# A first and a last batch with forms of their own, and new moments, in a four-layer graph network on one core

## The chip, the core and the metric

The kernel runs on one core of one Trainium2 chip. Five engines take part, each with a queue that it works through in order: PE (TensorE, matmuls), DVE (VectorE), ACT (ScalarE), POOL (GpSimd) and SP (SyncE, which here only issues transfers). Transfers are carried out by 16 DMA engines. The metric is the device time of one execution in microseconds (us), before the change 2229.95 us in the median of three runs.

## The reference

Sixteen batches of 1024 nodes with 64 channels pass through four graph layers. Each layer adds its result to its input and normalises over the channels:

```python
x = _layernorm(x + _L0_gnn_ref(x, adj, L0_gnn_weight, L0_gnn_bias), axis=-1)
x = _layernorm(x + _L1_gnn_ref(x, adj, L1_gnn_theta), axis=-1)
x = _layernorm(x + _L2_gnn_ref(x, adj, nodemask, L2_gnn_W1, ...), axis=-1)
x = _layernorm(x + _L3_gnn_ref(x, adj, L3_gnn_gamma, ...), axis=-1)
```

- Layer 0 is `adj @ (x @ weight) + bias`.
- Layer 1 is a Chebyshev sum of order four: `z0 = x`, `z1 = adj @ x`, `z(k) = 2 adj @ z(k-1) - z(k-2)`, each times its own `theta[k]`.
- Layer 2 drops some neighbours of nodes with many of them (`_dilate_adj`), sorts the remaining neighbours' values channel by channel, takes the quantiles 0.25, 0.5 and 0.75 by linear interpolation, weights and adds them, and sends the sum with `x` through a small perceptron (64 to 128 to 64).
- Layer 3 normalises over all batches and nodes at once, multiplies by `W`, and subtracts the product with `sqrt(d) * adj * rsqrt(d)`, where `d` are the row sums of `adj`.

About 0.8% of the adjacency is set, so a node has some nine neighbours. The kernel ranks the nodes by their number of neighbours, so that few nodes need a long sort.

## The kernel before

Nodes lie on the 128 partitions, eight groups of 128 to a batch (NK = 8). A batch goes through nine generators, each a function with `yield`s that cut it into steps:

- `rows_in` (11 steps): loads the adjacency in eight tiles of 128 rows (L405, SP's queue, two buffers), makes of each a key (ACT's Sign, L539, times a band on DVE, L541) whose eight largest per block (MAX8, L544) give the list of neighbours; `transposed` (L410 to L416) turns the tile on PE and ACT copies it into the transposed adjacency `f_adj_t`. After the last tile that adjacency is written out (4 MB, L565) and the first product with it is made.
- `layers` (13): layers 0 and 1. Layer 0's norm is eight squares with sums on ACT (L366), a root on ACT (L369), a reciprocal on DVE (L371, `n1_r`) and eight scalings on ACT (L376). Products with the adjacency are `hop2` (L385 to L396), 16 matmuls that the profile shows as 32 rows; ACT copies the result out (`f_ct`, L602). The last product's rows go to DRAM (`rows`, L630), from where they are gathered.
- `lists` (15): neighbours, gaps and ranks on DVE (L646 to L739), then for each of the eight groups a comparison (`at16`, L747) and the matmuls that place the lists (L751) and reorder the batch's own rows (L515, `reordered`); then ACT copies out `ids`, `more` and `meta` (L770 to L776) and the reordered rows (L785).
- `fetch` (15): 70 gathers per batch on POOL (L808), each followed by a memset (L811): 15 for class 0, 37 for class 1 and 18 for class 2.
- `heads` (10), three classes: nodes of one group with up to 24 slots (class 0), four groups with 11 (class 1), three with 8 (class 2). `dead` (L832) marks empty slots once the gathers have landed; ACT copies the gathered values into `home` and adds a huge number where the slot is empty (L880, 23, 40 and 21 instructions).
- `sorts` (141): a sorting network on DVE (L912) between the tiles `home` and `away`; then ACT multiplies the sorted slots by the quantile weights (L928) and PE adds them up (L929).
- `ends` (5): perceptron and layer 2's norm. Its product is scaled on ACT (L965), added on DVE (L966) and normalised as above (`n2`).
- `back` (11): brings the rows into the old order with eight comparisons on DVE (L993) and the matmuls of L515.
- `third` (5): the local part of layer 3. Step 1 turns the rows, copies them (L1011), takes statistics (bn_stats, L1014), multiplies by `rd` (L1019, `f_u`); step 2 is the product and ACT's copy of it (`f_ht`, L1025); steps 3 and 4 multiply by `sd` (L1030) and write out z (L1042).

A last stage over all batches (not in the diff) normalises and writes the output.

The order on the engines is written by hand. Each step has a due time in `WHEN`; step u of a part of batch b is due at `b * PERIOD + WHEN[part][u]` with PERIOD = 118, and all steps of all batches are sorted by that, ties in the order in which they were listed, which is by batch:

```python
parts += [(b * PERIOD + when, b, name, u, part) for u, when in enumerate(WHEN[name])]
for _, b, name, u, part in sorted(parts, key=lambda p: p[0]):
    next(part)
```

The due times are no times of the chip; they only settle the order in which instructions are put on the queues. Three or four batches are under way at once: batch b's tiles and its layers run while batch b-2 is sorted and batch b-3 is in `third`. A setup of weights and constants (`prepared`, L447 to L497) is cut into pieces that run after steps named in SETUP.

Of the kernel before, what the change touches and what calls it, by code (L numbers as in the profile page):

```python
# [10 lines left out]
F32 = mybir.dt.float32  # L11
BF16 = mybir.dt.bfloat16
F16 = mybir.dt.float16
# [3 lines left out]
ALU = mybir.AluOpType  # L17
# [25 lines left out]
SETUP = (("rows in", 8), ("rows in", 10), ("layers", 1))  # L43
# [135 lines left out]
def _strides(slots):  # L179

    out, rest = [], list(slots)
    while rest:
# [16 lines left out]
    "rows in": (-307.2, -238.7, -234, -231.9, -226.9, -224.5, -217, -214.8, -208.8, -202.9, -195.8),  # L199
    "layers": (-174.9, -126.5, -121.9, -119.7, -113.9, -113.5, -107.6, -104.6, -98.7, -96.7, -79.9, -79.6, -77.8),  # L200
    "lists": (-134.7, -132, -126.3, -126.3, -117.8, -76.3, -76.3, -74.6, -63.5, -63.4, -61.9, -57.9, -57.4, -45.7, -12.4),
    "fetch": (-18.6, -1.8, -1.8, 0.8, 0.8, 5.6, 24.5, 28.9, 28.9, 52.8, 56.1, 56.1, 79.5, 91.2, 92.5),
    "heads": (5.3, 15.7, 18.7, 67.9, 93.8, 93.8, 93.8, 115.1, 121.9, 126.8),
    "sorts": (
        23.2, 23.2, 23.2, 23.2, 23.2, 23.2, 23.2, 23.2, 23.2, 23.2, 23.2, 23.2, 24.8, 34.3, 38, 38.6, 38.7, 38.7,
        42.6, 42.6, 43.4, 43.4, 45.4, 45.4, 48.8, 49.7, 51, 51, 51.9, 51.9, 53.9, 55.5, 55.5, 55.5, 55.8, 57, 57,
        57, 57, 57, 57, 59.5, 59.5, 60.5, 61.9, 61.9, 61.9, 62.5, 62.5, 62.5, 62.5, 62.5, 62.5, 62.5, 62.5, 62.5,
        62.5, 62.5, 63.6, 63.6, 63.6, 68.3, 68.3, 70.5, 71.5, 73.4, 73.7, 77.1, 77.7, 79.1, 79.1, 79.1, 80.2, 80.2,
        89.2, 89.2, 93, 93.4, 93.4, 93.9, 102.3, 102.3, 102.3, 102.3, 102.3, 102.3, 109.8, 109.8, 110.3, 111.3,
        111.7, 111.9, 111.9, 111.9, 113.8, 113.8, 114.2, 114.2, 114.2, 114.4, 116.9, 117.4, 118.5, 118.6, 118.6,  # L210
        118.6, 118.6, 118.6, 118.6, 120, 121.7, 121.7, 121.7, 121.7, 121.7, 121.9, 121.9, 121.9, 121.9, 121.9,
        128.4, 128.4, 128.4, 128.4, 128.4, 128.4, 128.4, 128.4, 128.4, 128.9, 128.9, 128.9, 128.9, 133.1, 135.4,
        135.4, 135.4, 135.7, 135.7, 139.8, 140.7,
    ),
    "ends": (153.6, 155, 158.8, 173.2, 179),
    "back": (154.2, 174, 188, 189.1, 192.7, 197.9, 200.1, 209.6, 211.1, 212.5, 212.5),
    "third": (202.6, 227.3, 232.1, 236.9, 244.4),
# [4 lines left out]
def gnn_layers_kernel(  # L222
# [129 lines left out]
    def norm(wk, y, wholes, tag, centred=False):  # L352

        n = NK // len(wholes)
        part = lambda k: wholes[k // n][:, k % n, :]
        if not centred:
            s = wk.tile([P, NK], F32, name=f"{tag}_s")
            for i, t in enumerate(wholes):
                nc.vector.tensor_reduce(out=s[:, i * n : (i + 1) * n], in_=t, axis=AX.X, op=ALU.add)
            nm = wk.tile([P, NK], F32, name=f"{tag}_m")  # L360
            nc.vector.tensor_scalar(out=nm, in0=s, scalar1=-1.0 / C, scalar2=None, op0=ALU.mult)
        v = wk.tile([P, NK], F32, name=f"{tag}_v")
        for k in range(NK):
            sq = wk.tile([P, C], F32, name=f"{tag}_q")
            bias = 0.0 if centred else nm[:, k : k + 1]
            nc.scalar.activation(sq, part(k), AF.Square, bias=bias, scale=1.0, accum_out=v[:, k : k + 1])  # L366
        yield "square"
        sd = wk.tile([P, NK], F32, name=f"{tag}_d")
        nc.scalar.activation(sd, v, AF.Sqrt, bias=eps_s, scale=1.0 / C)  # L369
        rs = wk.tile([P, NK], F32, name=f"{tag}_r")  # L370
        nc.vector.reciprocal(rs, sd)  # L371
        if not centred:
            nc.vector.tensor_tensor(out=nm, in0=nm, in1=rs, op=ALU.mult)
        for k in range(NK):
            if centred:
                nc.scalar.mul(y[:, k, :], part(k), rs[:, k : k + 1])  # L376
            else:
                nc.scalar.activation(
                    y[:, k, :], part(k), AF.Identity, bias=nm[:, k : k + 1], scale=rs[:, k : k + 1]
                )  # L380
# [4 lines left out]
    def hop2(adj_t, v, ps):  # L385

        pairs = adj_t.rearrange("p j (q h n) -> p j h q n", h=2, n=P)
        for j in range(NK):
            for h in range(2):
                nc.tensor.matmul(  # L390
                    ps[h * C : (h + 1) * C, :],
                    lhsT=v[:, j, :],
                    rhs=pairs[:, j, h],
                    start=(j == 0),
                    stop=(j == NK - 1),
                )  # L396

    def turned(src, tag, bufs=1):

        pt = bank(tag, bufs)  # L400
        for q in range(NK // 2):
            nc.tensor.transpose(pt[:, q * P : (q + 1) * P], src[:, q * P : (q + 1) * P], ident)
        return pt

# [42 lines left out]
    def prepared(th, thp, mean, w0_c, left, mine, term):  # L447

        halves = [slice(h * C, (h + 1) * C) for h in range(2)]
        centred(mean, w0_c)  # L450
# [16 lines left out]
        nc.vector.tensor_copy(out=biases, in_=mine)  # L467
        yield

        nc.vector.tensor_copy(out=mask_f, in_=mask_u)  # L470
        pm = bank("end")
        nc.tensor.transpose(pm[:, 0:P], mask_f, ident)
        nc.vector.tensor_copy(out=mask_t, in_=pm[:, 0:P])
        nc.vector.tensor_copy(out=earlier, in_=earlier_f)
# [10 lines left out]
        centred(mean, thp)  # L485
        thf = bank("end").rearrange("p (k c) -> p k c", c=C)[:, 0:4]
# [36 lines left out]
    def rows_in(b, st, keyband, pa, pw):  # L523
# [7 lines left out]
        held = [load(b, i, pa) for i in range(2)]  # L531
        yield "load"
        for i in range(NK):
            a = held.pop(0)

            off = (NK - 1 - i) * P
            key = pa.tile([P, NK, P], F16, name="key", bufs=KEYS)
            flat_key = key.rearrange("p j n -> p (j n)")
            nc.scalar.activation(flat_key, a, AF.Sign)  # L539
            transposed(a, i, adj_t)  # L540
            nc.vector.tensor_tensor(out=flat_key, in0=flat_key, in1=keyband[:, off : off + N], op=ALU.mult)  # L541

            for j in range(NK):
                nc.vector.max(out=cand[:, i, j * 8 : j * 8 + 8], in_=key[:, j, :])  # L544
            left = cand[:, i, :]
            for r in range(KS // 8):
                top = lst[:, i, r * 8 : r * 8 + 8]
                nc.vector.max(out=top, in_=left)
                if r < KS // 8 - 1:
                    then = pa.tile([P, NK * 8], F16, name="then", bufs=2)  # L550
                    nc.vector.match_replace(out=then, in_to_replace=top, in_values=left, imm_value=0.0)
                    left = then
            if i + 2 < NK:
                held.append(load(b, i + 2, pa))
            yield f"tile{i}"
# [3 lines left out]
        q0 = bank("l0", 2)  # L559
        hop2(adj_t, x0, q0)  # L560
# [76 lines left out]
    def lists(b, st, pw):  # L637
# [105 lines left out]
        po = bank("px")  # L743
        pr, px = (pr[:, : NK * RW].rearrange("p (k s) -> p k s", s=RW), pr[:, NK * RW : (NK + 1) * RW])
        for k in range(NK):
# [21 lines left out]
            reordered(po, st["x_parts"], at_place[:, 0:N], k)  # L767
# [15 lines left out]
        yield "ids"  # L783
        own_t = pw.tile([P, N], F16, name="row").bitcast(F32)
# [32 lines left out]
    def heads(b, st, gots, pw, ps_):  # L817

        meta, xs = st["meta"], st["xs"]
        for ns, nr, _, ks in CLASSES:  # L820
# [50 lines left out]
            nc.scalar.copy(home[:, 0, :, :], xs[:, kk, :])  # L871
# [5 lines left out]
            for u, v in zip(cuts[:-1], cuts[1:]):  # L877
                for s in range(u, v):
# [10 lines left out]
    def sorts(b, st, ps_):  # L889

        xs = st["xs"]
        for (ns, nr, _, ks), (steps, homes) in zip(CLASSES, plans):
# [31 lines left out]
            for u, v in zip(*(np.linspace(0, nr, SUMS[k0] + 1).astype(int)[e] for e in (slice(0, -1), slice(1, None)))):  # L924
                for i in range(u, v):
                    t = home[homes[i]][:, i]
                    for k in range(nk):
                        nc.scalar.mul(t[:, k, :], t[:, k, :], wts[:, i, k : k + 1])  # L928
                    nc.tensor.matmul(total, lhsT=quarter, rhs=flat(t), start=False, stop=(i == nr - 1))  # L929
                yield f"sums{k0}"  # L930

    def ends(b, st, pw):
# [31 lines left out]
        for k in range(NK):  # L964
            nc.scalar.mul(h[:, k, :], ph[:, k * C : (k + 1) * C], meta[:, k, 1:2])  # L965
        nc.vector.tensor_tensor(out=h, in0=h, in1=xs, op=ALU.add)  # L966
        x3p = h
        yield from norm(pw, x3p, [h], "n2", centred=True)
# [3 lines left out]
    def back(b, st, pw):  # L972
# [4 lines left out]
        for g in range(2):  # L977
# [9 lines left out]
            nc.scalar.copy(row[:, g * 512 : (g + 1) * 512], ps)  # L987
            yield f"row{g}"
# [12 lines left out]
    def third(b, st, pa, pw):  # L1001
# [9 lines left out]
        nc.scalar.copy(flat(x3), turned(xt, "end"))  # L1011
        nc.sync.dma_start(out=x3_d[b], in_=flat(x3))
        st = pw.tile([P, 6], F32, name="f_st")
# [3 lines left out]
        u = pw.tile([P, NK, C], F32, name="f_u")  # L1017
        for k in range(NK):
            nc.scalar.mul(u[:, k, :], x3[:, k, :], rd[:, k : k + 1])  # L1019
        nc.scalar.copy(u[:, :, C - 1], rd)  # L1020
# [8 lines left out]
        for k in range(NK):  # L1029
            nc.scalar.mul(z[:, k, :], pq[:, k * C : (k + 1) * C], sd[:, k : k + 1])  # L1030
# [15 lines left out]
    with (  # L1046
# [28 lines left out]
        for b in range(B):  # L1075
            st = {}
            for name, part in (
# [10 lines left out]
                parts += [(b * PERIOD + when, b, name, u, part) for u, when in enumerate(WHEN[name])]  # L1088
# [691 lines left out]
```

## Time and profile before

| | us |
|---|---|
| three runs | 2225.72, 2229.95, 2231.18 |
| the profiled execution, its own time | 2228.49 |
| the profiled execution, its span | 2226.6 |
| first gather of batch 0 starts | 112.86 |
| first gather of batch 14 and of batch 15 | 1821.12, 1941.38 |
| last gather's memset | 2060.47 |
| last stage begins | about 2145 |

The granted TensorE clock of that execution was 0.857 on the mean. The page gives the busy time of each engine and, in 40 slices, its share in tenths. A line of the timeline has the start, the duration, the engine, the line and operation, the output and input tiles with their shapes, and in brackets the idle time just before, with what ended it. Lines of several like instructions in a row are put together (x8). In lists of waits the three numbers are the time in total, the number of times and the longest, in us. In tables of windows each engine has its busy time and the number of instructions, then come the granted PE clock, the DMA share and GB/s.

### The profile page before, as it was taken

The page shows a single profiled execution, that of the slowest core. Times are in us where ns is not written, and L with a number is a line of the kernel's source. Part 1 is how long each engine was busy: PE and PEld are TensorE (multiplying, and loading weights), DVE is VectorE, ACT ScalarE, POOL GpSimd, SP SyncE. Part 2 cuts the span into 40 slices and gives each one's busy share as a digit, 9 for nine tenths or more (in the row PEclk, how much of TensorE's full clock was granted, in tenths as well). Part 3 has the DMA queues.
Part 4 walks back from the last instruction along what each step waited for, and adds up shares of the span by engine and source line. Part 5 has one row for each costly group of instructions (what it writes and reads, how often), then busy time and mean ns, then how long its engine had stood idle before and what let it go on. Part 6 is the DMA issues. An engine that isn't in the chain of part 4 may idle for free. (4 is left out here: it accounts for less than half of the span.)

```text
span 2226.6 us, 35647 instructions
## 1 busy us (share of the span) xinstructions
PE 1677.5 (75%) x9926; PEld 955.8 (43%) x9926; DVE 1851.7 (83%) x5686; ACT 1480.2 (66%) x5397; POOL 1755.2 (79%) x2289
## 2 busy tenths in 40 slices
PE   5984787888787877888787877878787877665643
PEld 3443344454444344444444344444444343333323
DVE  7677988888889988898989988899889887667526
ACT  4463777677686777677686777677686776675523
POOL 1088989899989989888888989789898889999014
PEclk8996898989889898989998998988898899776765
DMA  5433262624436262624435262624435253131226
GB/s 201 160 115 89 68 209 68 201 73 132 127 82 205 72 210 68 199 71 132 133 83 193 73 208 68 198 76 143 119 82 193 73 185 104 26 105 25 81 83 156
DMA packets 129764, 272.42 MB, mean 122 GB/s; under 512 B 76324, under 2 KB 76500, under 8 KB 119316
## 3 DMA queue, kind: packets, MB, share of 16 engines
q1 hardware_dynamic: 57248, 218.40, 27.1%
q0 software_dynamic: 36160, 38.13, 10.3%
q10 hardware_dynamic: 36148, 13.53, 2.6%
q8 instruction: 80, 1.31, 0.3%
q14 instruction: 128, 1.05, 0.2%
HBM read 185.89 MB, written 84.07 MB: 121 GB/s over the span
## 5 line engine op out<-in xcount | busy, mean ns | idle before, releaser
L808 POOL DMA_INDIRECT got<-rows,ids x1072 | 1157.6, 1080 | 184.8 <-issue 126.0
L811 POOL MEMSET rest<- 128x384 f32 x1120 | 505.9, 452 | 0.7
L390 PE MATMUL ps_l<-f_adj_t,f_t 128*64 128x512 f32 x1536 | 347.6, 606 | 0.7 <-ACT f_t L608 0.7
L880 ACT ACTIVATE home<-got,big 128x64 f32<-128x64 f32 x1344 | 327.1, 333 | 0.4
L929 PE MATMUL ps_xt<-home,quarter 128*128 128x256 f32 (+2 forms) x672 | 214.8, 450 | 142.8 <-ACT home L928 133.6
L912 DVE TENSOR_TENSOR away<-home 128x768 f32<-128x768 f32 (+9 forms) x416 | 229.9, 575 | 54.3 <-PE ps_xt L929 48.7
L928 ACT ACTIVATE home<-home,wts 128x64 f32<-128x64 f32 x896 | 228.9, 338 | 7.3 <-DVE home L912 7.0
L929 PEld LDWEIGHTS ps_xt<-home,quarter 128*128 128x128 f32 x672 | 130.2, 249 | 219.9 <-ACT home L928 219.9
L544 DVE MAX8 cand<-key 128x8 f16<-128x128 f16 x1024 | 210.6, 278 | 4.4
L390 PEld LDWEIGHTS ps_l<-f_adj_t,f_t 128*64 128x64 f32 x1536 | 107.6, 140 | 210.6 <-issue 205.3
L415 PE MATMUL ps_turn<-cf,f_a 128*128 128x128 f32 x1024 | 155.9, 301 | 40.1 <-ACT f_adj_t L416 27.0
L912 DVE TENSOR_TENSOR home<-away,home 128x128 f32<-128x128 f32 (+5 forms) x352 | 166.4, 477 | 5.1
L808 POOL DMA_INDIRECT extra<-rows,more x48 | 50.8, 1058 | 150.0 <-DMA rows<-xr 122.6
L415 PEld LDWEIGHTS ps_turn<-cf,f_a 128*128 128x128 f32 x1024 | 124.3, 153 | 100.8 <-ACT f_adj_t L416 51.2
L515 PE MATMUL ps_end<-at,f_h 128*64 128x512 f16 x256 | 65.1, 481 | 115.8 <-DVE at L993 95.8
L912 DVE TENSOR_TENSOR home<-away 128x64 f32<-128x64 f32 (+7 forms) x304 | 149.1, 507 | 1.1
L416 ACT COPY f_adj_t<-ps_turn 128x512 f32<-128x512 f32 x256 | 137.3, 591 | 6.8 <-PE ps_turn L415 6.6
L539 ACT ACTIVATE key<-f_a 128x1024 f16<-128x1024 f32 x128 | 136.0, 1062 | 8.4 <-DMA f_a<-in_adj_dram 6.0
L541 DVE TENSOR_TENSOR key<-key,keyband 128x1024 f16<-128x1024 f16 x128 | 88.3, 690 | 57.7 <-ACT key L539 57.7
L390 PE MATMUL ps_end<-f_adj_t,f_u 128*64 128x512 f32 x512 | 122.4, 634 | 17.0 <-ACT f_u L1020 14.0
L602 ACT COPY f_ct<-ps_l 128x512 f32<-128x512 f32 x48 | 28.1, 585 | 156.8 <-PE ps_l L390 156.8
L912 DVE TENSOR_TENSOR home<-home 128x64 f32<-128x64 f32 (+7 forms) x240 | 120.0, 500 | 6.2
(254 smaller groups left out, 3533.3 us busy)
## 6 DMA issues: line engine op xcount, KB each, us to landing
f_a<-in_adj_dram SPq DMA_DIRECT2D x128, 512.0 KB
adj<-f_adj_t SPq DMA_DIRECT2D x16, 4096.0 KB
f_adj_t<-adj SPq DMA_DIRECT2D x64, 1024.0 KB
got<-rows,ids POOLq DMA_INDIRECT x1072
rows<-xr ACTq DMA_DIRECT2D x16, 264.0 KB
f_x<-in_x_dram ACTq DMA_DIRECT2D x16, 256.0 KB
x_d<-f_x SPq DMA_DIRECT2D x16, 256.0 KB
z_d<-f_ht SPq DMA_DIRECT2D x16, 256.0 KB
```

The costliest lines, as they stand in the source:

```text
L390: nc.tensor.matmul(ps[h * C : (h + 1) * C, :], lhsT=v[:, j, :], rhs=pairs[:, j, h], start=(j == 0), stop=(j == NK - 1),)
L415: nc.tensor.transpose(pt[:, j * P : (j + 1) * P], a[:, (4 * g + j) * P : (4 * g + j + 1) * P], ident)
L416: nc.scalar.copy(adj_t[:, 4 * g : 4 * g + 4, i * P : (i + 1) * P], pt.rearrange("p (j n) -> p j n", n=P))
L539: nc.scalar.activation(flat_key, a, AF.Sign)
L541: nc.vector.tensor_tensor(out=flat_key, in0=flat_key, in1=keyband[:, off : off + N], op=ALU.mult)
L544: nc.vector.max(out=cand[:, i, j * 8 : j * 8 + 8], in_=key[:, j, :])
L808: nc.gpsimd.indirect_dma_start(out=w[0], out_offset=None, in_=rows[:, :], in_offset=bass.IndirectOffsetOnAxis(ap=w[1], axis=0))
L811: nc.gpsimd.memset(rest, 0.0)
L880: nc.scalar.activation(home[:, s + 1, k, :], got[:, s, k, 0:C], AF.Identity, bias=big_dead[:, s, k : k + 1], scale=1.0,)
L912: nc.vector.tensor_tensor(out=at(ho, r1 if is_max else r0, *run), in0=at(ha, r0, *run), in1=at(hb, r1, *run), op=ALU.max if is_max else AL ...
L928: nc.scalar.mul(t[:, k, :], t[:, k, :], wts[:, i, k : k + 1])
L929: nc.tensor.matmul(total, lhsT=quarter, rhs=flat(t), start=False, stop=(i == nr - 1))
```

## The change

It has five pieces.

1. All due times are new (WHEN), and batches 0, 1, 14 and 15 have tables of their own (OWN), which the driver uses instead.
2. Batch 0's tiles are transposed before the key is made, and its first product is made by quarters of 128 columns, each as soon as its tiles are there. Setup is cut into four pieces, not three, and these run after other steps.
3. Batch 0's lists leave out the reorder matmuls in the loop; after `ids` the eight comparisons are made a second time, and the reorder follows.
4. Batch 15: the home copies are adds on DVE, two or three to a class; the last class's weights are applied on DVE; layer 2's scaling and norm run on DVE over the whole batch at once; 12 matmuls `warm` on constants follow the second row of `back`; `third` multiplies by `rd` and `sd` on DVE straight from PSUM.
5. In `third`, for all batches, the multiplications by `rd` stand ahead of the statistics and their two writes.

```diff
+WARM = 12
-SETUP = (("rows in", 8), ("rows in", 10), ("layers", 1))
+SETUP = (("rows in", 3), ("lists", 1), ("layers", 6), ("layers", 8))
...
-    "layers": (-174.9, -126.5, -121.9, -119.7, -113.9, -113.5, -107.6, -104.6, -98.7, -96.7, -79.9, -79.6, -77.8),
+    "layers": (-175.9, -122, -122, -120.6, -113.9, -113.5, -107.6, -102.5, -98.7, -96.6, -79.1, -79.1, -77),
...
-    "third": (202.6, 227.3, 232.1, 236.9, 244.4),
+    "third": (202.5, 227.2, 232, 237.3, 243.5),
...
+OWN[0] = {
...
+    "third": (191.9, 227, 233.2, 234.9, 245),
...
+OWN[1] = {
...
+    "third": (141.5, 227.7, 233.3, 234.2, 242.6),
...
+OWN[14] = {
...
+    "layers": (-190.9, -166.8, -122.9, -117, -113.5, -113.5, -108.3, -108.3, -96.8, -96.8, -69.5, -69.5, -69.5),
...
-    def norm(wk, y, wholes, tag, centred=False):
+    def norm(wk, y, wholes, tag, centred=False, whole=False):
+        if whole:
+            v = wk.tile([P, NK], F32, name=f"{tag}_v")
+            sq = wk.tile([P, NK, C], F32, name="x3_mid")
+            nc.vector.tensor_tensor(out=sq, in0=wholes[0], in1=wholes[0], op=ALU.mult)
+            nc.vector.tensor_reduce(out=v, in_=sq, axis=AX.X, op=ALU.add)
+            yield "square"
+            sd = wk.tile([P, NK], F32, name=f"{tag}_d")
+            nc.scalar.activation(sd, v, AF.Sqrt, bias=eps_s, scale=1.0 / C)
+            rs = wk.tile([P, NK], F32, name=f"{tag}_r")
+            nc.vector.reciprocal(rs, sd)
+            nc.vector.tensor_tensor(out=y, in0=wholes[0], in1=rows_by(y, rs), op=ALU.mult)
+            return
...
-    def hop2(adj_t, v, ps):
+    def hop2(adj_t, v, ps, q=None):
...
+    def warm(n):
+        pt = bank("turn", 2).rearrange("p (k n) -> p k n", n=P)
+        for _ in range(n):
+            nc.tensor.matmul(
+                pt, lhsT=ones_h, rhs=ones_h.unsqueeze(1).to_broadcast([P, 4, P]), start=True, stop=True
+            )
...
+            if b == 0:
+                transposed(a, i, adj_t)
+                if i > 1 and i % 2 == 0:
+                    hop2(adj_t, x0, q0, i // 2 - 1)
             nc.scalar.activation(flat_key, a, AF.Sign)
-            transposed(a, i, adj_t)
+            if b > 0:
+                transposed(a, i, adj_t)
...
-            reordered(po, st["x_parts"], at_place[:, 0:N], k)
+            if b > 0:
+                reordered(po, st["x_parts"], at_place[:, 0:N], k)
...
+        if b == 0:
+            po = bank("px")
+            for k in range(NK):
+                at_place = pw.tile([P, N + P], F16, name="at16", bufs=2)[:, 0:N]
+                nc.vector.tensor_scalar(
+                    out=at_place, in0=columns[:, 0:N], scalar1=place[:, k : k + 1], scalar2=None, op0=ALU.is_equal
+                )
+                reordered(po, st["x_parts"], at_place, k)
...
+                if b == B - 1:
+                    nc.vector.tensor_tensor(
+                        out=home[:, u + 1 : v + 1],
+                        in0=got[:, u:v, :, 0:C],
+                        in1=big_dead[:, u:v].unsqueeze(3).to_broadcast([P, v - u, nk, C]),
+                        op=ALU.add,
+                    )
...
+                    if b == B - 1 and k0 == CLASSES[-1][3][0]:
+                        nc.vector.tensor_tensor(out=t, in0=t, in1=rows_by(t, wts[:, i, :]), op=ALU.mult)
...
+        if b == B - 1:
+            nc.vector.tensor_tensor(
+                out=h, in0=ph.rearrange("p (k c) -> p k c", c=C), in1=rows_by(h, meta[:, :, 1]), op=ALU.mult
+            )
...
+            if g and b == B - 1:
+                warm(WARM)
...
+        if b == B - 1:
+            nc.vector.tensor_tensor(out=u, in0=pt.rearrange("p (k c) -> p k c", c=C), in1=rows_by(u, rd), op=ALU.mult)
...
+        if b == B - 1:
+            nc.vector.tensor_tensor(out=z, in0=pq.rearrange("p (k c) -> p k c", c=C), in1=rows_by(z, sd), op=ALU.mult)
...
-                parts += [(b * PERIOD + when, b, name, u, part) for u, when in enumerate(WHEN[name])]
+                parts += [(b * PERIOD + when, b, name, u, part) for u, when in enumerate(OWN.get(b, WHEN)[name])]
```

## The prediction

> **What bounds the kernel now.** I read the page's shares and slices first, then the windows of three periods in the middle, then who waits for whom on VectorE there, then the rows round those waits, and last the ramp and the tail.
>
> ```profile
> PE 1677.5 (75%) x9926; PEld 955.8 (43%) x9926; DVE 1851.7 (83%) x5686; ACT 1480.2 (66%) x5397; POOL 1755.2 (79%) x2289
> ...
> DVE  7677988888889988898989988899889887667526
> ACT  4463777677686777677686777677686776675523
> POOL 1088989899989989888888989789898889999014
> ```
>
> There are three stages. POOL does not gather in the first two slices, then POOL and DVE are both nearly full for 35 slices, and in the last three POOL has next to nothing. The middle looks bound by both engines, so a closer table is needed: three periods of one batch each.
>
> ```profile
> core 0: us, PE busy (x) PEld busy (x) DVE busy (x) ACT busy (x) POOL busy (x), PEclk, DMA share, GB/s
> 1178.60:1303.90 125.30, 100.39 (x616) 56.04 (x615) 112.88 (x347) 91.04 (x336) 108.88 (x143) 0.90 0.42 129
> 1303.90:1429.50 125.60, 101.41 (x612) 57.45 (x610) 111.42 (x347) 90.30 (x333) 106.87 (x141) 0.89 0.43 128
> ```
>
> A batch takes 125.3 us. POOL's own 70 gathers, at about 1.69 us from one to the next, need 118.3, and the memsets and issue are in that; so POOL has 7 us to spare and VectorE's order sets the pace: 112.1 us of work, 5 us of gaps under 0.3 us, and five waits.
>
> ```profile
> DVE n_r L371 <- ACT n_d L369: 8.0, 3, 3.7
> DVE key L541 <- ACT key L539: 7.7, 6, 2.3
> DVE x_mid L505 <- ACT f_h L376: 6.3, 3, 2.1
> DVE away L912 <- PE ps_xt L929: 2.0, 3, 0.7
> ```
>
> These are over those three periods: per batch 2.7, 2.6, 2.1 and 0.7 us, 8 in all. All of them are waits for ACT or PE, which are late because they waited for DVE before: the three engines hand one chain round, and a delay on it has nowhere to go. The place that matters most here is the norm of layer 0:
>
> ```profile
> 1231.31 0.59 ACT L1025 COPY f_ht<-ps_end 128x512 f32<-128x512 f32 x1 [4.55 <-PE ps_end L390]
> 1231.79 0.30 ACT L369 ACTIVATE n_d<-n_v,eps_s 128x8 f32<-128x8 f32 x1
> ...
> 1232.13 0.20 DVE L371 RECIPROCAL n_r<-n_d 128x8 f32<-128x8 f32 x1 [2.04 <-ACT n_d L369]
> ...
> 1264.64 7.09 PE L390 MATMUL ps_l<-f_adj_t,f_t 128*64 128x512 f32 x32
> ```
>
> ACT has finished the eight squares of that norm (L366, 1224.02 to 1226.75) and sits 4.55 us before f_ht, the copy of a product of the batch three earlier; only then comes the root, and DVE waits for it.
>
> **The change, part by part.** Nothing here is taken as faster because it is finer; each is placed on that chain.
>
> *General times, batches 5 to 13.* Step 2 of third and step 1 of layers now fall due at the same moment (232 less three periods is -122), and the earlier batch goes first. So the eight squares stand behind f_ht. In the row above they run in the 4.55 us idle time; after the change they begin at 1231.79 and take 2.73 us, and root and reciprocal come that much later. Something is given back: "dead" of class 1 (L832) moves ahead of some ten sort steps and the last three steps of the class-0 sort ahead of the 4.1 us of list work from L646 to L673, so the multiplications of that class lose their 0.53 us wait, and f_ht comes about 0.5 earlier. ACT's chain: 2.85 less 0.5, +2.35. DVE's reciprocal is also moved four sort steps forward (L912, 0.42 each): those 1.7 us now come after the wait and not in it. From there to the end of the class-1 sort DVE has no wait before the change (1232.25 to 1257.05) and ACT does wait for that sort (1.00 and 0.20), so the delay passes on whole: +4.05. Then the class-1 sums: PE does three of nine, the hop of 32 matmuls (L390), then six; ACT 12 multiplications, the copy f_ct (L602), 24. Counted from the end of the sort S: four multiplications (0.97) and a sum to S+1.75, hop 7.09 to S+8.85, copy, 24 times 0.2425 to S+15.2, key. Before, that key was at 1272.26, S+15.2: equal. But the next transposes wait for the last sums, and the home copies end at S+24.7 instead of S+24.1: +0.55. Sum per batch +4.6; nine batches, +41.4. Lower end: another order hides it all, 0. Upper end: with DVE's idle time at 6.1 us and nothing given back, 9 x 6 = 54.
>
> *The same hop's clock.* It now starts after PE has worked some 2.5 of 11 us (in the shifted rows), not after a run of sums. Hops of this shape take 7.09 us at best, 7.6 to 8.0 at 235, 361, 488, 614, 737 and 863, and 8.54 and 9.91 near the end, after thinly used stretches. Ends 0 and 2.82 a batch; I take the middle of the six, 0.75, since one sum still runs just before: ten batches, +7.5.
>
> *Own times of batches 0, 1, 14, 15.* Where third belongs to batch 0 or 1 or layers to batch 14, f_ht goes behind the norm altogether. The reciprocal loses its wait (2.04 to 4.26 us in the periods seen): three batches, 3 each, -9 (ends -4 and -13). Batch 15's own case lies under POOL's last two batches, 239.3 us of gathers back to back from batch 14's first (1821.12) to 2060.47, and gives nothing.
>
> *Ramp (batch 0's form).*
>
> ```profile
> 50.55 0.22 ACT L366 ACTIVATE n_q<-ps_l 128x64 f32<-128x64 f32 x1 [12.85 <-PE ps_l L586]
> ...
> 112.86 1.14 POOL L808 DMA_INDIRECT extra<-rows,more  x1 [99.22 <-DMA rows<-xr]
> ```
>
> Transposes before the key and the hop by quarters take the hop (29.20 to 37.1) off the path; the setup, 37.14 to 47.2 on DVE, is spread over the tiles, which end later by 3.3 (40.5 for 37.2). The norm's start goes from 50.55 to about 42.3, -8.3. The three hops of the layers are unchanged. The rows DMA was issued at 100.42 and landed only near 111.9, behind batch 1's 4 MB adjacency write (94.93) and two tile loads; that write moves by the tiles it follows, about -6.7, and it stays ahead. So I take -6.7 for the first gather and for batch 0's data, on which DVE waited 8.05 us at 200.67. The eight extra comparisons of the split product (128x1024, 0.49 each, 3.9 us) come behind ids, under the 8.05. Ends: -14 (the queue is gone too) and 0 (the wait at 200.67 takes it).
>
> In the case's rows, gathers beside such comparisons (1305 to 1316) take 0.95 to 1.39 us, away from them (1268 to 1282) 0.95 to 1.35: no price. [...]
>
> *Tail (batch 15's form).*
>
> ```profile
> 2052.59 1.49 DVE L912 TENSOR_TENSOR away<-home 128x1280 f32<-128x1280 f32 x1 [7.32 <-PE ps_xt L929]
> ...
> 2060.47 0.43 POOL L811 MEMSET rest<- 128x384 f32 x1
> ...
> 2121.88 9.91 PE L390 MATMUL ps_end<-f_adj_t,f_u 128*64 128x512 f32 x32 [2.96 <-ACT f_u L1020]
> ```
>
> The class-1 sort starts 7.3 us late and after 40 ACT home copies (9.64). With three adds on DVE (128x768 twice at 0.96, 128x1024 at 1.22) it starts near 2038; then class 2 is bound by its data, near 2063. From there: dead 1.35, two adds 1.75, last two sort steps 1.97, weights 0.23, class-2 sort 9.9 (as 2077.79 to 2087.67), seven multiplications of 128x192 at 0.36, one sum: 2081.8 where ACT saw 2092.87, -11. Ends: multiplication 1.75 to 0.69, squares 2.99 to 1.3, scaling 2.02 to 0.69 and less hand-over: -4.3. Step u: 2.02 and the 0.59 copy before it against 0.76: -1.85; z: -1.05. Warm matmuls: twelve at 0.21 to 0.43 in a 6.59 us gap of PE before 2110.07; the reorder's matmuls ran at 0.43 until 2113.9 and 0.21 after. Ends -2.3 and +1.8, taken -1. Sum -19.2 (ends -25 and -8).
>
> [...]
>
> *At nothing.* The four 1.39 us of got copies (L828) and the copy of z (L1042) move behind 12 home copies, so z's write stands 3 us later on SP's queue, ahead of tile loads. The cover is that key L539 waits for tiles 6.0 us in the whole run; without it, up to 3 a batch. The bn_stats writes keep their place. The third part's new order inside a step is the old one on ACT.
>
> Sum: -6.7 - 9 + 41.4 + 7.5 - 19.2 = +14. The profiled execution took 2228.49 (span 2226.6), the median is 1.46 above; on the median: 2244.
>
> **Rivals.**
> B, faster: the swap is absorbed. If the root's lateness meets ACT or DVE slack that I have not seen (the 4.43 us that ACT waits for dead at 1200.46 is the candidate, if PE's reorder also moves forward), swap and hop cost 5 in all: -30, 2200. Against it: f_x3t waits for PE, whose last comparison does not move. It decides if the reciprocal's wait stays under 3 us.
> C, slower still: the hop after three sums runs at 9.91: 10 x 2.82, 2265. For it: the thin PE before; against: the best case in 1264.64.
> D, both ends give their most (-14 and -25): 2231, no change.
>
> **How the numbers follow.** A 0.52, B 0.27, C 0.12, D 0.09. This kernel's measurement can tell 0.3% from no change, 6.7 us (2223.3 to 2236.6). A's own range, 2226 to 2262, gives 0.02 faster, 0.10 same, 0.40 slower; B 0.26 and 0.01; C 0.12 slower; D 0.02, 0.05, 0.02. Faster 0.30, same 0.16, slower 0.54. Range 2200 to 2265: half of B and of C lie outside.
>
> **What would show it.** Right: a period of 129 to 131 us in the middle, n_r L371 waiting 6 us for n_d in batches 5 to 13 and hardly in 3, 4 and 14, first gather near 106, last gather to end of the last back 20 us shorter. Wrong: a period of 126 or less, with f_ht early or n_r waiting 2 to 4 us as now.

## The result and the profile after

| | before | after |
|---|---|---|
| runs, median (us) | 2230.56, four runs, 2225.72 to 2235.16 | 2292.71, four runs, 2289.29 to 2293.87 |
| ratio of the times | | 1.0287, 95% interval 1.0257 to 1.0317 |
| span of the profiled execution | 2226.6 | 2292.0 |
| mean granted clock of TensorE | 0.857 | 0.847 |
| first gather of batch 0 starts | 112.86 | 112.00 |
| first gather of batch 14 and of batch 15 | 1821.12, 1941.38 | 1902.10, 2023.10 |
| last gather ends | 2060.5 | 2145.6 |
| from there to the end | 166.1 | 146.4 |

The change makes the kernel slower, on the side that was forecast, but by 62 us where 14 were forecast. The loss came before the last gather, and the end gained what was forecast. First the page's busy times and POOL's row of slices, after the change:

```profile
PE 1715.4 (75%) x10034; PEld 969.8 (42%) x10034; DVE 1872.8 (82%) x5714; ACT 1450.2 (63%) x5244; POOL 1745.5 (76%) x2289
...
POOL 1088889998987969698696968878685987999404
```

No engine has much more to do: DVE 21 us, PE 38, ACT 30 less, POOL 10 less. The span grew by 65 us all the same, and in the middle POOL's slices fall to 6 in 6 places where none of before's middle slices is under 7. So the added time is waiting, and it lies in the long middle. The table of windows shows it for three periods, from the rounding of one batch's `ids` to the next. The columns are those of the table before the change.

```profile
1238.30:1371.30 133.00, 103.70 (x618) 55.95 (x617) 111.88 (x346) 90.62 (x335) 104.75 (x140) 0.90 0.41 122
1371.30:1502.60 131.30, 101.40 (x612) 55.85 (x612) 112.08 (x346) 90.50 (x334) 105.34 (x140) 0.90 0.41 123
1502.60:1634.35 131.75, 102.35 (x612) 55.17 (x612) 111.80 (x346) 90.52 (x334) 106.00 (x140) 0.90 0.40 121
```

A period is 132.0 us in the mean of the three, where it was 125.3, with DVE's work the same to a microsecond. What DVE waits for in these three periods (total, times, longest) is:

```profile
DVE n_r L479 <- ACT n_d L477: 22.1, 3, 8.3
DVE key L667 <- ACT key L664: 14.6, 6, 4.2
DVE x_mid L624 <- ACT f_h L484: 8.3, 4, 2.1
DVE away L1060 <- PE ps_xt L1080: 2.0, 3, 0.7
```

The lines are renumbered: L479, L667, L624 and L1060 are L371, L541, L505 and L912 of before. The norm's wait went from 2.7 to 7.4 us a period and the wait for the key from 2.6 to 4.9. The other two did not grow (the window holds `x_mid` once more). These two account for 7.0 us; the period grew by 6.7. The timeline shows the norm of layer 0 in one of these periods:

```profile
1263.86 0.32 PE L858 MATMUL ps_l<-same,earlier 128*128 128x192 bf16 x1 [3.06 <-DVE same L851]
...
1265.95 9.02 PE L499 MATMUL ps_end<-f_adj_t,f_u 128*64 128x512 f32 x32
...
1275.02 0.58 ACT L1187 COPY f_ht<-ps_end 128x512 f32<-128x512 f32 x1 [11.27 <-PE ps_end L499]
1275.51 0.23 ACT L474 ACTIVATE n_q<-ps_l 128x64 f32<-128x64 f32 x1
...
1278.28 0.30 ACT L477 ACTIVATE n_d<-n_v,eps_s 128x8 f32<-128x8 f32 x1
1278.62 0.20 DVE L479 RECIPROCAL n_r<-n_d 128x8 f32<-128x8 f32 x1 [8.30 <-ACT n_d L477]
```

ACT sits idle for 11.27 us before `f_ht` (it was 4.55): the squares (2.7 us) now stand behind that copy, and ACT is there 3.7 us sooner after the period's `ids`. Only after the copy come the squares, the root and DVE's reciprocal. The hop that `f_ht` waits for is itself slower, 9.02 us, where the three of before in this stretch took 7.09, 7.09 and 7.67. PE had stood for 3.06 us just ahead of it: the matmuls of the ranks (L858) come first on its queue, and they wait for DVE.

The lateness against before, read at each batch's `ids`, gives a ledger of the two profiled executions:

| stretch | forecast | measured |
|---|---|---|
| start to `ids` of batch 2 | -6.7 | +6.7 |
| two periods, with the norms of batches 3 and 4 | -6 | +1.1 |
| nine periods, batches 5 to 13 | +48.9 | +68.5 |
| period with batch 14's own table | -3 | +4.7 |
| POOL's last two batches | 0 | +4.1 |
| last gather to the end | -19.2 | -19.7 |
| sum | +14 | +65.4 |

Of the 51 us between the two sums, 20 lie in the nine periods, 15 in the two rows with own tables, 13 in the ramp and 4 in POOL's last two batches. The last of the nine periods is 12.6 us longer than before, the other eight 7.0 each. Experiments 4, 6 and 12 below have that jump too (133.1, 133.7 and 129.7 us beside 126, 126 and 123), and experiment 7, without batch 14's table, does not (124.5). So some 5 us of the third row belong to that table.

### The profile page after: what moved, and what is told of

It reads as the page before. It is cut to its first block, busy times and chain, and to the rows that moved or that the text cites. A ratio compares the mean times of both kernels' runs of the same rounds, so it can differ in the third digit from the quotient of the medians.

```text
span 2292.0 us, 35744 instructions
## 1 busy us (share of the span) xinstructions
PE 1715.4 (75%) x10034; PEld 969.8 (42%) x10034; DVE 1872.8 (82%) x5714; ACT 1450.2 (63%) x5244; POOL 1745.5 (76%) x2289
## 5 line engine op out<-in xcount | busy, mean ns | idle before, releaser
L499 PE MATMUL ps_l<-f_adj_t,f_t 128*64 128x512 f32 x1536 | 366.2, 632 | 2.7 <-ACT f_t L737 2.7
L1080 PE MATMUL ps_xt<-home,quarter 128*128 128x256 f32 (+2 forms) x672 | 207.3, 423 | 138.6 <-ACT home L1079 135.1
L1028 ACT ACTIVATE home<-got,big 128x64 f32<-128x64 f32 x1260 | 306.3, 333 | 0.0
L1060 DVE TENSOR_TENSOR away<-home 128x768 f32<-128x768 f32 (+9 forms) x416 | 229.1, 573 | 37.1 <-PE ps_xt L1080 32.3
L1080 PEld LDWEIGHTS ps_xt<-home,quarter 128*128 128x128 f32 x672 | 119.0, 229 | 221.1 <-ACT home L1079 220.6
L532 PEld LDWEIGHTS ps_turn<-cf,f_a 128*128 128x128 f32 x1024 | 129.7, 156 | 103.0 <-ACT f_adj_t L533 43.1
L1060 DVE TENSOR_TENSOR home<-away,home 128x128 f32<-128x128 f32 (+5 forms) x352 | 165.2, 473 | 5.7
L1060 DVE TENSOR_TENSOR home<-away 128x64 f32<-128x64 f32 (+7 forms) x304 | 150.6, 509 | 1.1
L667 DVE TENSOR_TENSOR key<-key,keyband 128x1024 f16<-128x1024 f16 x128 | 87.8, 686 | 71.1 <-ACT key L664 70.9
L499 PE MATMUL ps_end<-f_adj_t,f_u 128*64 128x512 f32 x512 | 127.1, 654 | 12.0 <-ACT f_u L1178 11.1
L1060 DVE TENSOR_TENSOR home<-home 128x64 f32<-128x64 f32 (+7 forms) x240 | 120.0, 500 | 7.3
```

The lines of the kernel that those rows point to most:

```text
L499: nc.tensor.matmul(ps[h * C : (h + 1) * C, cols], lhsT=v[:, j, :], rhs=pairs[:, j, h, qs], start=(j == 0), stop=(j == NK - 1),)
L532: nc.tensor.transpose(pt[:, j * P : (j + 1) * P], a[:, (4 * g + j) * P : (4 * g + j + 1) * P], ident)
L1028: nc.scalar.activation(home[:, s + 1, k, :], got[:, s, k, 0:C], AF.Identity, bias=big_dead[:, s, k : k + 1], scale=1.0,)
L1060: nc.vector.tensor_tensor(out=at(ho, r1 if is_max else r0, *run), in0=at(ha, r0, *run), in1=at(hb, r1, *run), op=ALU.max if is_max else AL ...
```

## The experiments

Each ratio is to runs of the kernel before on the same chip. All times are medians in us.

**1. The squares of the norm ahead of the copy.** Only ACT's order changes, in nine batches.

```diff
-    "layers": (-175.9, -122, -122, -120.6, -113.9, -113.5, -107.6,
+    "layers": (-175.9, -122.05, -122, -120.6, -113.9, -113.5, -107.6,
```

> The changed kernel with step 1 of layers due 0.05 earlier, so that in batches 5 to 13 the eight squares of layer 0's norm stand ahead of f_ht on ACT again; nothing else moves on any engine (nine moves of one ACT copy). Theory (the swap is the larger part of the loss): the wait of n_r falls from 7.5 to about 4.7 us, 2.7 to 3.5 us a batch, 25 to 31 us in all, so about 2264 against 2292.7. Rival (the clock and the split sums set the period, the squares lie under something else): less than 8 us, 2285 or more.

Measured: 2264.07, ratio 1.0168 (1.0129 to 1.0206). The theory's time was hit. The norm's wait falls from 22.1 to 15.3 us over three periods, and the period from 132.0 to 129.7, by 2.3 us.

**2. The product after all nine sums, as before the change.**

```diff
-    "layers": (-175.9, -122, -122, -120.6, -113.9, -113.5, -107.6,
+    "layers": (-175.9, -122, -122, -120.6, -113.9, -113.5, -107.45,
```

> The changed kernel with step 6 of layers due 0.15 later, so that the product after the class-1 sums follows six of the nine sums (as two of the three parts) and not three. Theory (splitting the sums makes PE thin before the product, so it runs at a lower clock, and puts ACT's multiplications behind it): the wait of key falls from 5.1 towards 3 us, 1.5 to 2.5 us in ten batches, about 2272. Rival (the key comes at the same distance from the sort's end either way, as the rows of before gave): no change, 2288 to 2296.

The expectation speaks of six sums, but both remaining parts moved. Nine sums need 36 multiplications on ACT, and in the trace 4, 4 and these 28 come before the product's copy `f_ct`:

```profile
1287.84 6.79 ACT L1079 ACTIVATE home<-home,wts 128x64 f32<-128x64 f32 x28 [0.20 <-DVE home L1060]
1302.45 0.58 ACT L731 COPY f_ct<-ps_l 128x512 f32<-128x512 f32 x1 [7.82 <-PE ps_l L499]
```

So the experiment undoes the split as a whole. Measured: 2261.43, ratio 1.0168 (1.0121 to 1.0215), 11 us better than expected. Its waits over the three periods:

```profile
DVE n_r L479 <- ACT n_d L477: 20.8, 3, 7.2
DVE key L667 <- ACT key L664: 8.0, 6, 2.3
```

The key's wait is back where it was before the change. So what the split of the sums costs shows in the key's wait, not in the norm's, and it is about 2.2 us a period. The step had been given 1.3 (0.55 and 0.75 for the clock). The products of the Chebyshev layer, three hops a batch, also went from 7.80 us in the mean back to 7.29 (7.21 before). By the rows, the hop right behind the sums accounts for 1.4 us of that: 8.46 us in the mean of eight periods after the change, 7.09 in all eight here and before. The rest is the order or the other hops; this was not separated.

**3. Both.**

> Both moves together. If swap and split are two separate costs on one chain they add: about 45 us less, 2247. If one only uncovers the other: the larger of the two alone, 2262 or more.

Measured: 2244.1, ratio 1.0086 (1.0056 to 1.0116). The two edits alone gain 28.6 and 31.3 us, together 48.6: most of both adds up, some is the same time. Period 128.6.

**4. The general due times of before, all else as after.**

```diff
-    "layers": (-175.9, -122, -122, -120.6, -113.9, -113.5, -107.6, -102.5, -98.7, -96.6, -79.1, -79.1, -77),
+    "layers": (-174.9, -126.5, -121.9, -119.7, -113.9, -113.5, -107.6, -104.6, -98.7, -96.7, -79.9, -79.6, -77.8),
...
-    "third": (202.5, 227.2, 232, 237.3, 243.5),
+    "third": (202.6, 227.3, 232.1, 236.9, 244.4),
```

> The changed kernel with the general due times of before; the forms and the four tables of batches 0, 1, 14 and 15 stay. Theory (the new general times cost what the periods of batches 5 to 13 show, 68 us): about 2222. Rival (the tables of the four batches and the forms carry a good part, through what they leave to the batches between): 2245 or more.

Measured: 2268.12, ratio 1.0168 (1.0116 to 1.0219). My theory, that the general times carry nearly all of the loss, fell. The windows of a middle period and of two late ones show where the rest lies:

```profile
1196.00:1322.00 126.00, 103.06 (x611) 59.65 (x611) 111.37 (x347) 89.90 (x334) 105.56 (x141) 0.88 0.43 128
1600.00:1733.00 133.00, 106.01 (x633) 59.37 (x630) 113.97 (x349) 93.57 (x347) 106.97 (x140) 0.87 0.43 132
1733.00:1865.00 132.00, 102.91 (x612) 57.39 (x612) 110.11 (x344) 89.22 (x323) 94.20 (x124) 0.86 0.36 110
```

The middle runs at 126 again, but the stretches where a batch with its own table meets batches with the general one take 132 and 133. Read at `ids`, 24 us are lost by batch 3, and from batch 12 to 15 another 30.

**5. Batch 15's forms alone.** Of the change only pieces 4 and 5 stay: no own tables, old due times, old setup, batch 0 as before.

```diff
-SETUP = (("rows in", 3), ("lists", 1), ("layers", 6), ("layers", 8))
+SETUP = (("rows in", 8), ("rows in", 10), ("layers", 1))
...
-            if b == 0:
+            if b == -1:
...
+OWN = {b: OWN[b] for b in ()}
```

> The kernel before with batch 15's forms alone (adds and multiplications on DVE, whole norm, warm matmuls, third's new order), all due times, setup and batch 0 as before. Theory (the forms give what lies on the path after the last gather, and the early start of the class-1 sort comes partly from the order): 10 to 14 us less than before, about 2217. Rival (the forms give the whole 19.7 us of the end without any table): about 2209.

Measured: 2215.79, ratio 0.9968 (0.9937 to 1.0). As expected: the forms shorten the end, from 166.1 to 157.9 us after the last gather. The edge of the interval touches no change.

**6. With the tables of batches 14 and 15.**

```diff
-OWN = {b: OWN[b] for b in ()}
+OWN = {b: OWN[b] for b in (14, 15)}
```

> The same with the two tables of batches 14 and 15 added. Theory (the seam between the general order and these tables costs, as periods 12 and 13 of 133.1 and 131.4 us beside 125.9 showed with the old general times): the end gains 16 to 20 us and the seam takes 13 to 15 before it, so about 2226, no better than the forms alone. Rival (the seam was due to batches 0 and 1): 2205 to 2210.

Measured: 2234.1, ratio 1.0049 (1.0028 to 1.0069). The two tables cost what they bring and more. The end after the last gather shrinks further, to 148.2, but periods 12, 13 and 14 take 133.7, 131.3 and 127.3 where they took 124.6, 124.7 and 113.1 before the change (period 12 runs from the `ids` of batch 12 to those of batch 13), and the last gather ends 29.9 us later than before.

**7. Batch 15's table alone,** to see which of the two makes that seam.

```diff
-OWN = {b: OWN[b] for b in ()}
+OWN = {b: OWN[b] for b in (15,)}
```

> The kernel before with batch 15's forms and table, batch 14 in the general times. Theory (the seam is where batch 14's table meets the general order, in the two periods before its gathers): the periods 12 and 13 are back at 125, the end keeps most of its 16 to 20 us, about 2210. Rival (batch 15's table makes the seam): 2228 or more, with periods 12 and 13 above 130.

Measured: 2253.78, ratio 1.0116 (1.0097 to 1.0135): in time the theory fell and its rival held. The periods divide the seam: period 12 is back at 124.5, so its 133.7 came from batch 14's table, and period 13 takes 136.6, which is batch 15's. The end keeps nothing: 161.6 us after the last gather, where the forms alone had 157.9. Against batches with general times, batch 15's table costs more than both tables together. In the window from 1690 to 1825, most of period 13, DVE's longest waits are:

```profile
DVE away L1058 <- PE ps_xt L1078: 6.5, 1, 6.5
DVE key L665 <- ACT key L662: 5.7, 1, 5.7
DVE n_r L479 <- ACT n_d L477: 5.4, 2, 4.7
```

In the same window before the change these were 0.7, 2.6 and 2.2. No single wait carries it: three handovers are later. I read this as the steps of the last batch's table falling in other places among those of its neighbours; which step it is was not tried.

**8. Batch 0's forms, the new setup, and the tables of batches 0 and 1,** on the kernel before.

```diff
-                if b == B - 1:
+                if b == B:
...
+OWN = {b: OWN[b] for b in (0, 1)}
```

> The kernel before with batch 0's forms, the new setup and the tables of batches 0 and 1; all else as before. Theory (the ramp's gain is given back, and more, where the tables of 0 and 1 meet the general order, as the 24 us lag at batch 3 with the old general times showed): 20 to 25 us slower than before, about 2251. Rival (batch 0's forms gain 6.7 us at the first gather and keep it): about 2221.

Measured: 2252.12, ratio 1.0136 (1.0093 to 1.0179), as expected. Periods 0 to 2 take 97.8, 125.2 and 136.5 us, and the 24 us by which batch 3's `ids` come late stay to the end.

**9. The same with batch 0's table alone.**

```diff
-OWN = {b: OWN[b] for b in (0, 1)}
+OWN = {b: OWN[b] for b in (0,)}
```

> The kernel before with batch 0's forms, the new setup and the table of batch 0, batch 1 in the general times. Theory (batch 1's table holds up the lists of batch 1 and the period after it, 136.5 us beside 126.5): ids of batch 1 near 190, period 2 at 126 to 128, the kernel within 5 us of before, 2221 to 2231. Rival (the new setup and batch 0's own order cost it): 2245 or more.

Measured: 2239.33, ratio 1.0054 (1.0032 to 1.0076), between the two theories: batch 1's table costs 13 us by the medians, 18 by the ratios, and the rest stays with batch 0's table, its forms and the setup. The `ids` of batch 1 come at 203.0, where about 190 were expected, 12 us later than before, though batch 1 has the general times. Batch 0's forms were not run without a table, so their own worth is open.

**10. Experiment 3, and the reciprocal back behind one of the four sort steps.**

```diff
-    "layers": (-175.9, -122.05, -122, -120.6, -113.9, -113.5, -107.45,
+    "layers": (-175.9, -122.05, -121.7, -120.6, -113.9, -113.5, -107.45,
```

> The changed kernel with squares first and sums first, and step 2 of layers due 0.3 later, which puts the reciprocal n_r behind four more steps of the class-1 sort on DVE, as before. Theory (the four steps of 1.7 us behind the wait are what is left of the loss in the middle): the wait of n_r falls from 4.9 to about 3, the period from 128 to 126, 15 to 18 us in nine batches, so about 2227. Rival (the wait only moves): 2240 to 2246.

The expectation speaks of four steps. The trace shows that the reciprocal passed one: before the change ten sort steps stand between the last list instruction and the reciprocal, after it six, and here seven, of which this is the seventh:

```profile
1238.66 0.69 DVE L1060 TENSOR_TENSOR away<-home 128x512 f32<-128x512 f32 x1
1242.60 0.20 DVE L479 RECIPROCAL n_r<-n_d 128x8 f32<-128x8 f32 x1 [3.25 <-ACT n_d L477]
```

Measured: 2235.84, ratio 1.0046 (1.0028 to 1.0065), by the medians 8 us less than experiment 3, half of what was expected of four steps. The period goes from 128.6 to 127.3 and the norm's wait from 16.0 to 12.0 over the three periods. The profiled execution is the slowest of the ten, 2244.33, and over the eight periods before batch 12's `ids` its gain is 0.5 a period, so the 1.3 is rough.

**11. The opposite order: the copy behind the whole norm.** The kernel of experiment 5, with `f_ht` after root and scalings of the norm on ACT, in 13 places. DVE's and PE's orders stay.

```diff
-    "third": (202.6, 227.3, 232.1, 236.9, 244.4),
+    "third": (202.6, 227.3, 232.3, 236.9, 244.4),
```

> The kernel before with batch 15's forms, and step 2 of third due 0.2 later, which puts f_ht behind the whole norm of layer 0 on ACT in thirteen places; no other engine's order moves. Theory (what costs is any norm instruction behind f_ht, so taking root and scaling from behind it gains too): n_r stops waiting (2 to 4 us, now under 0.7), the period falls from 125.2 to about 123, 18 to 22 us less than batch 15's forms alone, about 2196. Rival (f_ht, now 1 us later, holds up the rest of third, and the wait comes back there): 2211 to 2220.

Measured: 2189.7 (2188.63 to 2192.45), ratio 0.9825 (0.9811 to 0.984): faster than both kernels and than was expected. The same place in its timeline:

```profile
1205.83 7.09 PE L499 MATMUL ps_end<-f_adj_t,f_u 128*64 128x512 f32 x32 [0.81 <-ACT f_u L1176]
...
1208.44 0.30 ACT L477 ACTIVATE n_d<-n_v,eps_s 128x8 f32<-128x8 f32 x1
...
1211.53 0.20 DVE L479 RECIPROCAL n_r<-n_d 128x8 f32<-128x8 f32 x1
```

The root ends 2.8 us before DVE comes to its reciprocal, while the hop for `f_ht` still runs. The list of DVE's waits has no line for `n_r` any more, and a period takes 122.8 us. Since experiment 5 differs from it in this order alone, the norm's place behind that copy cost the kernel before about 2 us a batch.

**12. The changed kernel with both cures.** The sums as in experiment 2 and the copy as in 11; own tables and all forms stay.

```diff
-    "layers": (-175.9, -122, -122, -120.6, -113.9, -113.5, -107.6,
+    "layers": (-175.9, -122, -122, -120.6, -113.9, -113.5, -107.45,
...
-    "third": (202.5, 227.2, 232, 237.3, 243.5),
+    "third": (202.5, 227.2, 232.3, 237.3, 243.5),
```

> The changed kernel with the product after six of the nine class-1 sums, and f_ht behind the whole norm of layer 0 in batches 5 to 13 (step 2 of third due 0.3 later; ACT's order alone moves by that). Theory (the two places in the general times make the loss of the middle, the four tables make the rest): n_r no longer waits in periods 4 to 12, these take 123 to 125 us, and the kernel lands where the tables' own loss and the end's gain leave it, 2215 to 2222. Rival (something else of the new general times holds the middle at 127 to 128): 2235 to 2244.

Measured: 2207.51, ratio 0.9906 (0.9883 to 0.9928). Two due times out of some hundreds take 85 us out of the changed kernel. The time is 8 us below the expected range. Its periods are 123.3 us up to batch 12's `ids`. It stays 18 us behind experiment 11. By the two profiles 10 of these are there by the `ids` of batch 4, 4 come in the next eight periods, 9 in the three after them and 9 in the last batch's gathers, and the end gives 13 back. All four tables together so cost less here than they did among the old general times (experiments 6 and 8).

## Why the prediction was right and wrong

**The swap: right in mechanism, too small in size.** The squares behind `f_ht`, the reciprocal forward, the split of the sums and the hop's clock were forecast at 5.35 us for each of nine batches. Measured were 6.7 in the three periods above and 7.0 in the eight that have no table's seam. DVE's waits divide the 6.7: the norm's grew by 4.7 (forecast 2.35 and 1.7, so 4.05), the key's by 2.3 (forecast 0.55 and 0.75, so 1.3). Term by term:

- *The squares behind f_ht, 2.85 before the 0.5 is taken off.* Experiment 1 undoes this alone and gains 2.3 a period in the three periods, 2.7 over all nine. Near.
- *"f_ht comes about 0.5 earlier".* It does, by more. In the mean of eight periods the copy starts 35.5 us after the period's `ids`, where it started 36.4 before; the hop starts 1.5 sooner and takes 0.5 longer.
- *Four sort steps behind the wait, +1.7.* Mis-sized: two of the four are of 128x512 and take 0.69, not 0.42, and all four take 2.0. DVE also comes to the reciprocal another 0.9 sooner after `ids` (31.9 for 34.8 us), which the sum did not have. Experiment 10 puts one step back. Three are left behind the wait, 1.3 us by its rows, and the norm's wait is still 1.3 a period above before (12.0 against 8.0 over three). The other 0.7 of its period (127.3 for 125.2) is busy time of DVE itself, 112.7 for 112.0, without a cause looked for.
- *The split of the sums, +0.55, and "the same hop's clock", +0.75.* This term was the furthest off in the general times. Experiment 2 undoes both and gains 2.3 a period. I took 0.75 for the hop behind the three sums, the middle of six; it lost 1.37 (7.09 to 8.46 us in the mean of eight periods; the one at 1307.91, of 8.53 us, had a granted clock of 0.63 in its first 4 us, where the one at 1264.64 before had 1.00 throughout). Layer 1's first hop lost 0.33 and the one for `f_ht` 0.49 (7.34 to 7.83), for which I had nothing; the other two of the five kept 7.09.

The hop for `f_ht` is uneven after the change. It took 7.09 us in the four of eight periods where PE came to the ranks' matmuls (L858) without a pause, and 7.46 to 9.02 in the four where it had stood 2.3 to 3.1 us there for DVE. Before the change pauses of up to 2.2 us stood there with hops of 7.09 to 8.49, so this pause alone does not settle it, and no run took it away. Experiment 12 shows that what is left of the loss goes through the norm's wait: with `f_ht` behind the norm its period is 123.3, only 0.5 above that of experiment 11 with the old due times.

**The own tables, -9: the step that failed by sign.** The norm's wait does vanish in batches 4 and 14 (4.17 and 2.17 us before), where f_ht now stands behind the norm; in batch 3 2.26 of 4.14 are left. This reading was right in the main, and experiment 11 gave it to all batches for 26 us by the medians. But I read each table only for the one handover that it mends, and took nothing for where its other steps fall among the neighbours' steps. For batches 3, 4 and 14 the stretches came out at +5.8 instead of -9. Experiments 6 to 9 show the price: among the old general times the two tables at the end cost some 18 us net of what they gain (0.9968 against 1.0049), batch 1's 13 to 18. Which of their steps does it was not tried. In the period with batch 14's norm an 8.33 us wait of DVE's `away` for `ps_xt` stands in its place.

**"I take -6.7 for the first gather": failed.** The norm of batch 0 starts at 41.55, as forecast (42.3). The timeline shows what came next:

```profile
37.58 0.33 SPq L694 DMA_DIRECT2D adj<-f_adj_t  x1
38.02 49.75 SPq L524 DMA_DIRECT2D f_a<-in_adj_dram  x8
...
41.55 0.22 ACT L474 ACTIVATE n_q<-ps_l 128x64 f32<-128x64 f32 x1 [1.70 <-PE ps_l L715]
...
52.96 1.06 ACT L664 ACTIVATE key<-f_a 128x1024 f16<-128x1024 f32 x1 [4.80 <-DMA f_a<-in_adj_dram]
```

Batch 1's first tile is loaded from 38.02 on, right behind batch 0's 4 MB write, and ACT and PE stand until 52.96 for it (4.80 and 11.46 us). That the write holds the load up is my reading of the order of the two; the profile does not show when the load landed. Of the 9 us that the norm was early, 3.4 are left at the end of the next hop. By the time of `ids` 1.4 are left (108.99 for 110.39), and of the first gather 0.86. The prediction asked what stands behind batch 1's write at 94.93, and not what stands behind batch 0's, which goes out at 37.58 for 30.46 before. From there the lag grows to +14.5 at the `ids` of batch 1 and falls to +6.7 at batch 2's. Experiment 9 has 12.3 of the 14.5 without batch 1's table, so that part lies with batch 0's table, its forms or the setup, and stays open.

**The end, -19.2: right as a sum,** -19.7, and in part by luck. From the last gather to the end of the class-2 sums 8.3 us were gained, where 11 were forecast. The reorder and the hop behind it gained 3.2, where the warm matmuls had 1, and the stretch behind that hop 2.7, where z had 1.05. Experiments 5 and 6 divide it: the forms give 8.3, batch 15's and 14's tables about as much again. The warm matmuls stand right ahead of the reorder:

```profile
2183.26 0.41 PE L634 MATMUL ps_end<-at,f_h 128*64 128x512 f16 x2
...
2191.97 8.52 PE L499 MATMUL ps_end<-f_adj_t,f_u 128*64 128x512 f32 x32 [1.64 <-ACT f_u L1178]
```

Each pair of the reorder takes 0.41 us from the first on, at a granted clock of 1.00 from 2183 to 2191 (0.64 to 0.66 until 2113.9 before, at 0.50). DVE's waits between the comparisons are 1.6 us in sum, where they were 3.5. The hop that follows takes 8.52 for 9.91. The worth of the warm matmuls by themselves, forecast at -1 between -2.3 and +1.8, no run shows.

**At nothing.** Nothing of the moved copies of L828 and L1042 shows among the waits. POOL's last two batches took 243.5 us where I had put 239.3: the gathers took 1103 and 1147 ns in the mean, for 1096 and 1097. No cause was looked for.

**The rivals.** B, the swap absorbed, is refuted by experiments 1 to 3, which find every part of it on the path. C named the right place, the clock of the hop after the split, but at 9.91 us, where it took 8.46. D's end gains came, without its ramp.

## What to carry to other kernels

Where three engines hand one chain round, ask of every in-order queue which instruction with a late input stands ahead of one that is ready, and move the late one back, even past work that looks less urgent; one copy in 13 places was worth some 26 us here. A table of due times that is right for one batch is not right next to other batches: price every handover that its steps pass, not only the one that it was made for. When a run of matmuls is split to start something sooner, price the clock of every product behind it (the next hop took 8.46 us here, for 7.09). And when an experiment moves a due time, count in the trace what really moved.

## What the runs showed of the hardware

TensorE's clock shows inside one product. The weight loads of the hop at 1265.95, after the change, follow one another like this (start, duration, and idle time before):

```profile
1266.86 0.24 PEld L499 LDWEIGHTS ps_end<-f_adj_t,f_u 128*64 128x64 f32 x2 [0.61 <-issue]
1267.72 0.24 PEld L499 LDWEIGHTS ps_end<-f_adj_t,f_u 128*64 128x64 f32 x2 [0.62 <-issue]
...
1270.09 0.14 PEld L499 LDWEIGHTS ps_end<-f_adj_t,f_u 128*64 128x64 f32 x2 [0.43 <-issue]
1270.52 0.14 PEld L499 LDWEIGHTS ps_end<-f_adj_t,f_u 128*64 128x64 f32 x2 [0.29 <-issue]
```

For the first 4.1 us a step takes 0.86, then 0.43. The granted clock in the tables of windows was 0.51 from 1266 to 1270 and 1.00 from 1270 to 1275. The slow steps take a little less than half of the hop's 9.02 us, and against a hop of 7.09 it loses 1.9 us by them. The hop at 1224.17, before the change, steps by 0.43 from 1224.66 to its end, at a granted clock of 1.00 from 1224 to 1232, and takes 7.09.

ACT kept the order of its queue here: it stood 11.27 us before `f_ht` at 1275.02, while the squares behind that copy, which read a product that PE had finished by 1236.95 (L715), needed nothing of it. They began at 1275.51. What experiment 11 gained by the order alone, 26 us by the medians against experiment 5, agrees.
